# Routing of the second layer with the norm in the row tile, scaling after the ranks and loads one step earlier

## The chip, the cores and the metric

The kernel runs on one core of a Trainium2 chip, as one launch. The metric is the device time of the launch in microseconds (us); the time before is the median of three runs. The engines are TensorE (PE, with its weight loads PEld), VectorE (DVE), ScalarE (ACT), GpSimd (POOL) and SyncE (SP), which issues most of the DMAs.

## What is computed

32 sequences of 256 rows of 128 numbers, 8192 rows in all, pass two layers, all in 32-bit floats. Each layer is `x = x + s * silu(m)`, where `s` is an attention block and `m` a mixture of experts, both of the normed rows.

```
xn = layernorm(x); s = softmax_transformer(xn)          # layer 0, two sublayers
x  = x + s * silu(top8_experts(xn) + shared(xn))        # 64 experts, 64 places each
xn = layernorm(x); s = linear_attention(xn)             # layer 1
topk_ids = argmax(xn @ gate_w); score = sigmoid(max(xn @ gate_w))
g  = silu(shared1(xn) + expert[topk_ids](xn * score))   # 32 experts, one per row
x  = x + s * g
```

The change lies between the two layers and in layer 1: the sum of layer 0, the second layernorm, the choice of the expert (argmax, score), the rank of each row within its expert, and the k and v of the linear attention.

## The kernel before

The rows are worked on in 16 groups (`NG`) of 512 rows, each as four tiles of 128 rows (`GT`). `s_rows` holds for every row 129 numbers: 128 for the row and its own number; `s_all` is the view of the 128.

The kernel has four stages. (1) Layer 0 (L309 to L799) runs in a loop over steps `k` from 0 to 17; in every step several generators are advanced in turn (`run`), so that attention, feed-forward, experts and shared expert are written interleaved. (2) The routing of layer 1 is a generator per group, `begin(g)`: `route(g)` (L178 to L244), followed for groups from 6 (`INL`) by the shared expert `shared1(g)` (L246 to L276). `rolling` runs the groups staggered, a new one after every two steps. Part of it is taken inside steps 15, 16 and 17 of layer 0: 10, 20 and 12 steps (L796 to L798). What is left is drained at L821, after layer 0. (3) Then the place of each row among 96 tiles of experts is computed (`dest`, L824 to L854), and `send` scatters 64 tiles of rows by GpSimd's indirect DMA (L860), while the linear attention (`linear_attention`, L873 to L957) begins. (4) `routed` loads the scattered rows, multiplies them by the experts' weights (L972, L982) and scatters them back (L987), beside the rest of the attention. At the end `finish` adds all up.

`route(g)` has five steps. Step 1 (L182 to L199) loads the two partial sums of the experts and of the shared expert of layer 0 (`c_g`, L185, tag "gate"; `c_m`, L187, tag "chan"), adds them on GpSimd (L188), loads the input rows x (L189), applies silu (by tanh for groups under 8, L192 to L194; as Silu after, L196 and L197) and adds to x (L198). Step 2 norms the rows into a tile `c_xn` of tag "tok": statistics on VectorE (L109, L110), small steps on GpSimd (L111 to L120), the rows on ScalarE (L122). Step 3 transposes them on TensorE (L132) and copies them from PSUM (L204). Step 4 has the logits (L208), the maximum and its index for each row (L216, L217), the mark of the chosen expert `hot` (L221) and the tanh of the score (L223). Step 5 finishes the score (L225), scales the normed rows by it into `s_rows` on GpSimd (L227, four instructions) and computes the ranks (L231 to L243, with the matmuls L235, L236 and L239).

Working tiles come from two pools. `works[0]` has one buffer per tag, `works[1]` two (score and others as noted). Groups 0 to 3 use `works[0]`; later ones use `works[0]` if g is a multiple of 3, and `works[1]` otherwise. Tag "out" is used by `shared1` for its result `f_y`, which ScalarE evicts (L274) and SP stores (L275). The rooms for x of groups 9 to 15 (`room`, L812) are in a pool that takes memory which layer 0 has used, as are the weights of layer 1 (`sw_a`, loaded at L805).

What sets the order: each engine has one queue and takes it in order, and a DMA that must wait on SP holds what stands behind it. The order within a queue is made when the program is built, by a planner that takes the written order as priority but puts ahead what it holds to be ready sooner. So it is near the written order and not the same: six loads of x stand in a row on SP, and the sum of group 15 (L188 at 881.6 us) stands ahead of seven groups' scalings (L227).

In `linear_attention`, k and v of each tile come out of one matmul group of 512 columns (L895) and are evicted with their bias by two VectorE instructions of 256 columns (L896 for `l_k`, L897 for `l_v`). Then follow Silu (L907), the square (L910), its sum per head (L911) and the scaling of k (L917) before the matmuls of L924.

Of the kernel before, what the change touches and what calls it, by code (L numbers as in the profile page):

```python
# [16 lines left out]
F32 = mybir.dt.float32  # L17
I32 = mybir.dt.int32
U32 = mybir.dt.uint32
AF = mybir.ActivationFunctionType  # L20
ALU = mybir.AluOpType
# [4 lines left out]
P = 128  # L26
BATCH, SEQ, D = 32, 256, 128
T = BATCH * SEQ
NT = T // P
GT = 4  # L30
NG = NT // GT
# [4 lines left out]
H1, D1, O1 = 16, 8, 2  # L36
# [24 lines left out]
def recurrent_kernel(ctx: ExitStack, tc: tile.TileContext, x, consts, small0, wsd, wgu, wd, small1, bias1, wr, out):  # L61
    nc = tc.nc
    vec, act, pool, pe, sp = nc.vector, nc.scalar, nc.gpsimd, nc.tensor, nc.sync

    def bcast(ap, axis, n):
        ap = ap.unsqueeze(axis)
        return ap.broadcast_to([n if i == axis else s for i, s in enumerate(ap.shape)])
# [16 lines left out]
    def rows(ap, g):  # L84
        return ap[g * GW : (g + 1) * GW].rearrange("(t p) d -> p t d", p=P)
# [3 lines left out]
    s_all = s_rows[:, :, :D]  # L89
# [8 lines left out]
    half = keep.tile([P, 1], F32, name="half")  # L98
# [29 lines left out]
    def transposed(src):  # L128

        ps = bank("tr", 2)  # L130
        for j in range(GT):
            pe.transpose(ps[:, j * P : (j + 1) * P], src[:, j], ident)  # L132
        return ps
# [11 lines left out]
    at1, x_at, xt_at, hots = {}, {}, {}, {}  # L145
# [6 lines left out]
    def room(pool_, gs):  # L152
        for g in gs:
            x_at[g] = pool_.tile([P, GT, D], F32, name=f"x_{g}")
            xt_at[g] = pool_.tile([P, GW], F32, name=f"xt_{g}")
            if g % 4 == 0:
                hots[g // 4] = pool_.tile([P, NT // 4, E1], F32, name=f"hot_{g // 4}")
# [18 lines left out]
    def work(n):  # L176

        return works[len(works) > 1 and n % 3 > 0]  # L178

    def route(g):  # L180

        wk = works[0] if g < EARLY else work(g)  # L182
        tl = slice(g * GT, (g + 1) * GT)
        gr = wk.tile([P, GT, D], F32, tag="gate", name="c_g")
        sp.dma_start(gr, rows(moe0[0], g))  # L185
        more = wk.tile([P, GT, D], F32, tag="chan", name="c_m")
        sp.dma_start(more, rows(moe0[1], g))  # L187
        pool.tensor_tensor(gr, gr, more, ALU.add)  # L188
        sp.dma_start(x_at[g], rows(x, g))  # L189
        if g < TANH:  # L190

            act.activation(more, gr, AF.Tanh, scale=0.5)  # L192
            vec.scalar_tensor_tensor(gr, more, 1.0, gr, ALU.add, ALU.mult)
            vec.scalar_tensor_tensor(gr, gr, 0.5, s_all[:, tl], ALU.mult, ALU.mult)  # L194
        else:
            act.activation(gr, gr, AF.Silu)  # L196
            vec.tensor_tensor(gr, gr, s_all[:, tl], ALU.mult)  # L197
        vec.tensor_tensor(x_at[g], x_at[g], gr, ALU.add)  # L198
        yield  # L199
        xn = wk.tile([P, GT, D], F32, tag="tok", name="c_xn")  # L200
        normed(wk, x_at[g], xn, act)
        yield
        ps = transposed(xn)
        act.copy(xt_at[g], ps)  # L204
        yield
        lp = bank()
        for j in range(GT):
            pe.matmul(  # L208
                lp[:, j * E1 : (j + 1) * E1], xt_at[g][:, j * P : (j + 1) * P], par1("router"),
                start=True, stop=True,  # L210
            )
        lg = lp[:, : GT * E1].rearrange("p (t e) -> p t e", e=E1)
        m8 = wk.tile([P, GT, 8], F32, name="c_m8")
        i8 = wk.tile([P, GT, 8], U32, name="c_i8")
        for j in range(GT):
            vec.max(m8[:, j], lg[:, j])  # L216
            vec.max_index(i8[:, j], m8[:, j], lg[:, j])  # L217
        fi = wk.tile([P, GT], F32, name="c_fi")
        vec.tensor_copy(fi, i8[:, :, 0])
        hot = hot_of(g)  # L220
        vec.tensor_tensor(hot, bcast(at1["eiota"], 1, GT), bcast(fi, 2, E1), ALU.is_equal)  # L221
        score = wk.tile([P, GT], F32, name="c_sc")
        act.activation(score, m8[:, :, 0], AF.Tanh, scale=0.5)  # L223
        yield
        vec.tensor_scalar(score, score, 0.5, 0.5, ALU.mult, ALU.add)  # L225
        for j in range(GT):
            pool.tensor_scalar(s_all[:, g * GT + j], xn[:, j], score[:, j : j + 1], 0.0, ALU.mult, ALU.add)  # L227


        cum = wk.tile([P, GT, E1], F32, name="c_cum")  # L230
        vec.tensor_copy(cum[:, 0], hot[:, 0])  # L231
        for j in range(1, GT):
            vec.tensor_tensor(cum[:, j], cum[:, j - 1], hot[:, j], ALU.add)
        ps = bank()
        pe.matmul(ps[:, : GT * E1], const("tri"), hot.rearrange("p t e -> p (t e)"), start=True, stop=False)  # L235
        pe.matmul(  # L236
            ps[:, E1 : GT * E1], at1["ones"], cum[:, : GT - 1].rearrange("p t e -> p (t e)"), start=False, stop=True,
        )
        pe.matmul(ps[:, GT * E1 : (GT + 1) * E1], at1["ones"], cum[:, GT - 1], start=True, stop=True)  # L239
        vec.tensor_tensor(at1["before"][:, g + 1], at1["before"][:, g], ps[:, GT * E1 : (GT + 1) * E1], ALU.add)  # L240
        pos = wk.tile([P, GT, E1], F32, name="c_pos")
        vec.tensor_tensor(pos, ps[:, : GT * E1].rearrange("p (t e) -> p t e", e=E1), hot, ALU.mult)
        vec.tensor_reduce(at1["rank"][:, tl], pos, AX.X, ALU.add)  # L243
        yield  # L244

    def shared1(g, home=None):  # L246
# [39 lines left out]
    def drain(i):  # L286
        for _ in i:
            pass
# [20 lines left out]
    with ExitStack() as c0:  # L309
# [3 lines left out]
        wk = c0.enter_context(tc.tile_pool(name="wk0", bufs=2, side="right"))  # L313
# [465 lines left out]
        begun = rolling([begin(g) for g in range(NG)], 2)  # L779
        for k in range(units + 2):  # L780
            if k == 9:
                cf.close()
                works.append(ctx.enter_context(tc.tile_pool(name="first_work", bufs=1)))
                begin1(ctx.enter_context(tc.tile_pool(name="first", bufs=1)))
            if k == 16:
                ca.close()
                works.append(ctx.enter_context(tc.tile_pool(name="mid_work", bufs=2)))
                room(ctx.enter_context(tc.tile_pool(name="mid", bufs=1)), range(EARLY, 9))
            steps = [beside(k), front(k), search(k), share(k)]

            qs = range(sum(working[: max(0, k - FIRST)]), sum(working[: max(0, k - FIRST + 1)]))
            steps += [chain(*(experts(q) for q in qs[i::2])) for i in range(2)]
            if k < units:
                gs, l = unit(k)
                steps = [softmax(gs, l, qkv, k < 9), *steps]
            more = {15: 10, 16: 20, 17: 12}.get(k)  # L796
            if more:
                steps.append(some(begun, more))  # L798
            drain(run(*steps))  # L799


    w1p = ctx.enter_context(tc.tile_pool(name="w1", bufs=1))
    wk = ctx.enter_context(tc.tile_pool(name="wk1", bufs=2))
    t = at1["sw_a"] = w1p.tile([P, cut], F32, name="sw_a")
    sp.dma_start(t, small1[:, :cut])  # L805
    bias = w1p.tile([P, 5 * D], F32, name="bias1")
    sp.dma_start(bias, bias1.broadcast_to([P, 5 * D]))

    vec.tensor_tensor(par1("wq"), par1("wq"), ident, ALU.add)
    wkv4 = par1("wkv").rearrange("p (k d) -> p k d", d=D)  # L810
    vec.tensor_tensor(wkv4, wkv4, bcast(ident, 1, 4), ALU.add)
    room(w1p, range(9, NG))  # L812
    before, rank, ones = at1["before"], at1["rank"], at1["ones"]

    spare = w1p.tile([P, S1], F32, name="spare")
    pool.iota(spare, [[P, S1]], base=T + 1, channel_multiplier=1, allow_small_or_imprecise_dtypes=True)
    siota = w1p.tile([P, 1], F32, name="siota")
    pool.iota(siota, [[0, 1]], base=0, channel_multiplier=P, allow_small_or_imprecise_dtypes=True)

    drain(begun)  # L820


    dest = w1p.tile([P, NT], I32, name="dest")
# [17 lines left out]
    ps = bank()  # L841
# [31 lines left out]
    def linear_attention(g):  # L873

        xt = xt_at[g]
        ps = bank()
# [6 lines left out]
        ps = bank()  # L883
# [3 lines left out]
        qn, kn = norms[:, : GT * H1], norms[:, GT * H1 :]  # L887
        vec.tensor_copy(qn, ps[:, : GT * H1])
        yield

        kf = wk.tile([P, GT, O1 * D], F32, name="l_k")
        vf = wk.tile([P, GT, O1 * D], F32, name="l_v")
        for j in range(GT):
            ps = bank("sc", 4)
            pe.matmul(ps, xt[:, j * P : (j + 1) * P], par1("wkv"), start=True, stop=True)  # L895
            vec.tensor_tensor(kf[:, j], ps[:, : O1 * D], bias[:, : O1 * D], ALU.add)  # L896
            vec.tensor_tensor(vf[:, j], ps[:, O1 * D :], bias[:, O1 * D : 2 * O1 * D], ALU.add)  # L897
            if j % 2:
                yield

# [5 lines left out]
            sp.dma_start(home, rows(moe1, g))  # L906
        act.activation(kf, kf, AF.Silu)  # L907
        k2 = work(g).tile([P, GT * O1 * H1, D1], F32, tag="wide", name="l_k2", bufs=1)
        kflat = kf.rearrange("p t (h d) -> p (t h) d", d=D1)
        act.activation(k2, kflat, AF.Square, bias=half)  # L910
        vec.tensor_reduce(kn, k2, AX.X, ALU.add)  # L911
        next(later, None)
        yield
        act.activation(norms, norms, AF.Sqrt)
        vec.tensor_scalar(norms, norms, 1e-6, None, ALU.add)
        vec.reciprocal(norms, norms)
        vec.scalar_tensor_tensor(kflat, kflat, 0.5, bcast(kn, 2, D1), ALU.add, ALU.mult)  # L917
        next(later, None)
        yield
        ps = bank("tr", 2)  # L920
# [13 lines left out]
        ps = bank()  # L934
# [11 lines left out]
        ps = transposed(o)  # L946
# [3 lines left out]
        ps = bank()  # L950
# [187 lines left out]
```

## Time and profile before

| | before |
|---|---|
| median of 3 runs | 1338.09 us (1333.77 to 1339.4) |
| profiled execution | 1336.66 us, of which the span from first to last instruction is 1334.9 us |
| mean granted TensorE clock | 0.972 |
| PE busy / share of the span | 1222.2 us, 92% |
| DVE, ACT, POOL busy | 943.5 us (71%), 787.6 us (59%), 650.6 us (49%) |
| first and last scatter of the rows (L860) | 942.3 us, 1045.4 us |
| last addition of layer 0 (L688) | 849.3 us |

How to read the profile: it is one execution. The table of stretches gives each engine's busy time in a stretch. A row of waits reads "who, which tile, which line, waited for whom: us in total, how often, the longest". The chain of work that ended last is followed back from the last instruction, at each step to what released it; its rows are start, duration, engine, tile and line. A row of groups gives line, engine and operation, the tiles written and read, their shapes, how often, the busy time in us and the mean of one in ns, and the idle time before it. The granted clock is the share of full speed that TensorE was given.

### The profile page before, as it was taken

How to read it: one execution, taken by the hardware profiler on the slowest of the kernel's cores; microseconds unless marked ns; L12 is line 12 of the kernel's file. 1: busy time of each engine (PE TensorE's matmuls, PEld its weight loads, DVE VectorE, ACT ScalarE, POOL GpSimd, SP SyncE). 2: the span in 40 equal slices, each digit the busy share in tenths (PEclk: the TensorE clock that was granted, in tenths of full speed). 3: DMA queues.
4: the chain of work that ended last, by engine and by line, in shares of the span. 5: the costliest groups of instructions: out<-in, count | busy, mean ns of one | idle time of the engine just before them, and what ended most of it. 6: DMA issues, size and time to landing. Idle time of an engine off the chain costs nothing. (4 is left out here: it accounts for less than half of the span.)

```text
span 1334.9 us, 22827 instructions
## 1 busy us (share of the span) xinstructions
PE 1222.2 (92%) x7425; PEld 863.2 (65%) x7425; DVE 943.5 (71%) x3064; ACT 787.6 (59%) x1858; POOL 650.6 (49%) x1020
## 2 busy tenths in 40 slices
PE   6989999999999899999998877889999899999997
PEld 4546576566566476667666545566566688888873
DVE  4699779879879856656655766776878666676537
ACT  1786666676676567676765766444545465564543
POOL 6362822733722557656644456252477434444540
PEclk9999999999999999999999998989989899999999
DMA  6020301311211332132211133311311366767767
GB/s 183 22 56 25 112 24 48 113 31 41 96 33 40 112 76 59 34 84 56 65 20 34 36 99 94 93 49 40 113 42 45 101 206 199 220 200 220 225 218 207
DMA packets 135078, 125.80 MB, mean 94 GB/s; under 512 B 17104, under 2 KB 110256, under 8 KB 134832
## 3 DMA queue, kind: packets, MB, share of 16 engines
q1 hardware_dynamic: 123696, 108.57, 27.4%
q0 software_dynamic: 11264, 15.78, 4.9%
q8 instruction: 59, 0.97, 0.3%
q14 instruction: 59, 0.48, 0.1%
HBM read 83.63 MB, written 40.68 MB: 93 GB/s over the span
## 5 line engine op out<-in xcount | busy, mean ns | idle before, releaser
L601 ACT ACTIVATE a_pr<-ps_sc,a_nm 128x256 f32<-128x256 f32 x256 | 119.4, 480 | 58.9 <-DVE a_nm L592 58.8
L987 POOL DMA_INDIRECT back<-e_ys,e_toi x96 | 95.1, 991 | 106.3 <-ACT e_ys L986 73.2
L111 POOL TENSOR_SCALAR bn_rs<-bn_mv 128x4 f32<-128x4 f32 x112 | 27.9, 249 | 230.4 <-DVE bn_mv L110 207.0
L663 PE MATMUL ps_mm<-xt,sw 128*128 128x512 f32 x256 | 135.4, 636 | 1.6 <-ACT e_y L523 0.9
L125 POOL TENSOR_SCALAR z<-s_rows,bn_rs 128x128 f32<-128x128 f32 x256 | 129.3, 526 | 6.6
L681 PE MATMUL ps_mm<-sw,m_h 128*128 128x128 f32 x1024 | 128.3, 280 | 2.2 <-ACT e_y L523 1.3
L681 PEld LDWEIGHTS ps_mm<-sw,m_h 128*128 128x128 f32 x1024 | 119.9, 193 | 12.7 <-issue 6.0
L668 DVE SCALAR_TENSOR_TENSOR m_h<-m_h,m_z 128x512 f32<-128x512 f32 x128 | 90.4, 710 | 46.4 <-ACT m_h L667 45.9
L112 POOL TENSOR_TENSOR bn_rs<-bn_rs,power 128x4 f32<-128x4 f32 x112 | 117.4, 1048 | 1.2
L665 ACT ACTIVATE m_z<-ps_mm,fold 128x512 f32<-128x512 f32 x128 | 87.4, 686 | 30.2 <-PE ps_mm L663 29.9
L592 DVE TENSOR_REDUCE a_nm<-ps_sc 128x2 f32<-128x512 f32 x128 | 83.3, 679 | 30.6 <-PE ps_sc L586 30.5
L972 PE MATMUL ps_sc<-e_xt,e_w 128*128 128x128 f32 x768 | 100.8, 278 | 1.0 <-ACT e_xt L1009 0.6
L972 PEld LDWEIGHTS ps_sc<-e_xt,e_w 128*128 128x128 f32 x768 | 94.5, 194 | 9.8 <-issue 7.8
L586 PE MATMUL ps_sc<-a_qk,a_qk 64*128 64x256 f32 x512 | 96.4, 411 | 1.2 <-ACT a_pr L601 1.1
L524 POOL DMA_INDIRECT sums<-e_y,sidx x32 | 51.1, 1598 | 80.4 <-ACT e_y L523 42.7
L618 PE MATMUL ps_tr<-con,a_pr 128*128 128x128 f32 x512 | 76.2, 279 | 9.5 <-ACT a_pt L619 5.6
L618 PEld LDWEIGHTS ps_tr<-con,a_pr 128*128 128x128 f32 x512 | 59.5, 144 | 38.3 <-issue 20.2
L667 ACT ACTIVATE m_h<-m_z 128x512 f32<-128x512 f32 x128 | 80.8, 635 | 1.7
L860 POOL DMA_INDIRECT xslot<-s_rows,dest x64 | 68.4, 1069 | 24.1 <-issue 18.5
L619 ACT COPY a_pt<-ps_tr 128x512 f32<-128x512 f32 x128 | 71.9, 591 | 12.4 <-PE ps_tr L618 11.4
L558 PE MATMUL ps_mm<-xt,sw 128*128 128x512 f32 x128 | 70.3, 657 | 6.4 <-ACT xt L546 3.0
L627 PE MATMUL ps_mm<-a_pt,a_v 128*64 128x256 f32 x512 | 70.9, 396 | 4.2 <-ACT m_z L665 3.6
(236 smaller groups left out, 2950.4 us busy)
## 6 DMA issues: line engine op xcount, KB each, us to landing
e_w<-in_wr_dram SPq DMA_DIRECT2D x96, 384.0 KB, 4.0
xslot<-zero SPq DMA_DIRECT2D x4, 1548.0 KB, 6.7
e_x<-xslot SPq DMA_DIRECT2D x24, 258.0 KB, 3.6
e_wg<-in_wgu_dram SPq DMA_DIRECT2D x16, 384.0 KB, 3.2
x_in<-in_x_dram SPq DMA_DIRECT2D x16, 256.0 KB, 3.2
tab<-s_rows SPq DMA_DIRECT2D x16, 256.0 KB, 2.4
sums<-s_y SPq DMA_DIRECT2D x16, 256.0 KB, 2.3
sums<-zero SPq DMA_DIRECT2D x4, 1024.0 KB, 8.4
```

The costliest lines, as they stand in the source:

```text
L112: pool.tensor_tensor(rs[:, 0], rs[:, 0], power, ALU.pow)
L125: ins = pool.tensor_scalar(dst[:, j], src[:, j], rs[:, 1, j : j + 1], rs[:, 0, j : j + 1], ALU.add, ALU.mult)
L586: pe.matmul(sc[h][:, j * SEQ : (j + 1) * SEQ], qk[0][hd, q0 : q0 + P], qk[1][hd, b * SEQ : (b + 1) * SEQ], start=True, stop=True,)
L592: vec.tensor_reduce(nm[:, 2 * h : 2 * h + 2], sc[h].rearrange("p (j k) -> p j k", k=SEQ), AX.X, ALU.max, negate=True)
L601: act.activation(pr[:, n], sc[h][:, j * SEQ : (j + 1) * SEQ], AF.Exp, bias=nm[:, n : n + 1], accum_out=su[:, n : n + 1],)
L618: pe.transpose(pts[:, n * P : (n + 1) * P], pr[:, n, k * P : (k + 1) * P], ident)
L663: pe.matmul(ps, par("w1", l * FF0 + f * P, P), xt, start=True, stop=True)
L665: act.activation(z, ps, AF.Identity, bias=fold[:, l, 3 + f : 4 + f])
L668: vec.scalar_tensor_tensor(h, h, 1.0, z, ALU.add, ALU.mult)
L681: pe.matmul(ps[:, j * D : (j + 1) * D], hs[f][:, j * P : (j + 1) * P], par("w2", l * FF0 + f * D, D), start=f == 0, stop=f == 3,)
L972: pe.matmul(ps[:, c * P : (c + 1) * P], wt[:, c * P : (c + 1) * P], xt, start=True, stop=True)
L987: ins = pool.indirect_dma_start(out=back, out_offset=bass.IndirectOffsetOnAxis(ap=to, axis=0), in_=ys, in_offset=None,)
```

## The change

Five things are changed.

1. `route(g)`: the two sums are loaded and added one step before they are used (a `yield` moves up), and odd groups use the tags "gate" and "chan", even groups "tok" and "out".
2. The normed rows are written into the row tile `s_rows` itself (no tile `c_xn`), and are scaled there in place by the score, in a step of its own after the ranks. The score gets three buffers.
3. 12, 24 and 16 steps are taken inside layer 0 for 10, 20 and 12; a group has now one step more.
4. The rest is drained before the identity is added to the weights of the attention, and before two small iotas.
5. k and v share one tile `l_kv`, evicted by one instruction of 512 columns; the later instructions read k from it with gaps.

```diff
@@ route
-        gr = wk.tile([P, GT, D], F32, tag="gate", name="c_g")
+        tags = ("gate", "chan") if g % 2 else ("tok", "out")
+        gr = wk.tile([P, GT, D], F32, tag=tags[0], name="c_g")
         sp.dma_start(gr, rows(moe0[0], g))
-        more = wk.tile([P, GT, D], F32, tag="chan", name="c_m")
+        more = wk.tile([P, GT, D], F32, tag=tags[1], name="c_m")
         sp.dma_start(more, rows(moe0[1], g))
         pool.tensor_tensor(gr, gr, more, ALU.add)
         sp.dma_start(x_at[g], rows(x, g))
+        yield
...
         vec.tensor_tensor(x_at[g], x_at[g], gr, ALU.add)
-        yield
-        xn = wk.tile([P, GT, D], F32, tag="tok", name="c_xn")
+        xn = s_all[:, tl]
         normed(wk, x_at[g], xn, act)
...
-        score = wk.tile([P, GT], F32, name="c_sc")
+        score = wk.tile([P, GT], F32, name="c_sc", bufs=3)
...
         vec.tensor_scalar(score, score, 0.5, 0.5, ALU.mult, ALU.add)
-        for j in range(GT):
-            pool.tensor_scalar(s_all[:, g * GT + j], xn[:, j], score[:, j : j + 1], 0.0, ALU.mult, ALU.add)
...
         vec.tensor_reduce(at1["rank"][:, tl], pos, AX.X, ALU.add)
+        yield
+        for j in range(GT):
+            pool.tensor_scalar(xn[:, j], xn[:, j], score[:, j : j + 1], 0.0, ALU.mult, ALU.add)
         yield
@@ layer 0's loop
-            more = {15: 10, 16: 20, 17: 12}.get(k)
+            more = {15: 12, 16: 24, 17: 16}.get(k)
@@ after layer 0
+    room(w1p, range(9, NG))
+    before, rank, ones = at1["before"], at1["rank"], at1["ones"]
+    drain(begun)
     vec.tensor_tensor(par1("wq"), par1("wq"), ident, ALU.add)
     wkv4 = par1("wkv").rearrange("p (k d) -> p k d", d=D)
     vec.tensor_tensor(wkv4, wkv4, bcast(ident, 1, 4), ALU.add)
-    room(w1p, range(9, NG))
-    before, rank, ones = at1["before"], at1["rank"], at1["ones"]
...
-    drain(begun)
@@ linear_attention
-        kf = wk.tile([P, GT, O1 * D], F32, name="l_k")
-        vf = wk.tile([P, GT, O1 * D], F32, name="l_v")
+        kv = wk.tile([P, GT, 2 * O1 * D], F32, name="l_kv")
+        kf, vf = kv[:, :, : O1 * D], kv[:, :, O1 * D :]
...
-            vec.tensor_tensor(kf[:, j], ps[:, : O1 * D], bias[:, : O1 * D], ALU.add)
-            vec.tensor_tensor(vf[:, j], ps[:, O1 * D :], bias[:, O1 * D : 2 * O1 * D], ALU.add)
+            vec.tensor_tensor(kv[:, j], ps, bias[:, : 2 * O1 * D], ALU.add)
...
-        kflat = kf.rearrange("p t (h d) -> p (t h) d", d=D1)
-        act.activation(k2, kflat, AF.Square, bias=half)
+        act.activation(k2.rearrange("p (t n) d -> p t (n d)", t=GT), kf, AF.Square, bias=half)
...
-        vec.scalar_tensor_tensor(kflat, kflat, 0.5, bcast(kn, 2, D1), ALU.add, ALU.mult)
+        k4 = kf.rearrange("p t (h d) -> p t h d", d=D1)
+        vec.scalar_tensor_tensor(k4, k4, 0.5, bcast(kn.rearrange("p (t h) -> p t h", t=GT), 3, D1), ALU.add, ALU.mult)
```

## The prediction, made before the changed kernel ran

> **What bounds the kernel now.** I read first the page's forty slices, for the granted clock, then the busy time by stage, then the waits of TensorE and ScalarE in the stretch the change is about, then the chain through the longest of those waits, and last the groups of the attention's evictions.
>
> From the table of busy time by stretch (start and end in us, then PE, PEld, DVE, ACT, POOL busy, granted clock, DMA share, GB/s):
>
> ```profile
> 700.00:800.00 100.00, 83.05 (x506) 55.99 (x502) 66.33 (x221) 62.80 (x159) 47.72 (x75) 0.93 0.21 54
> 800.00:850.00 50.00, 40.15 (x230) 30.75 (x231) 33.27 (x143) 27.57 (x56) 24.69 (x42) 0.87 0.23 68
> 850.00:900.00 50.00, 41.63 (x181) 27.27 (x181) 36.41 (x205) 20.61 (x47) 26.19 (x48) 0.86 0.34 94
> 900.00:950.00 50.00, 46.96 (x266) 33.21 (x265) 37.09 (x177) 20.39 (x42) 16.94 (x35) 1.00 0.24 72
> 1100.00:1150.00 50.00, 47.34 (x354) 41.03 (x353) 34.99 (x105) 29.34 (x62) 23.04 (x28) 1.00 0.70 209
> ```
>
> TensorE carries the kernel: 47 of 50 us in the last stage. Only from 720 to 890 us is it clearly idle (16.95 us in 700 to 800, 9.85 in 800 to 850, 8.37 in 850 to 900), and there its clock is low too. In this stretch layer 0 ends and the routing of layer 1 (L178 to L244) runs in its shadow until 849.3 us, then alone with the shared expert until 942.3 us, when the first scatter of L860 starts. So the change can win at most what TensorE loses in this stretch, and a little later.
>
> The waits there, who for whom, us in total, times, longest; first for 700 to 850 us, then for 840 to 945 us:
>
> ```profile
> PE ps_tr L132 <- ACT c_xn L122: 9.5, 4, 6.8
> ACT c_xn L122 <- POOL s_rows L227: 11.1, 5, 3.5
> ```
>
> ```profile
> PE ps_tr L132 <- ACT c_xn L122: 2.0, 3, 1.1
> ACT c_xn L122 <- POOL s_rows L227: 14.5, 7, 3.3
> POOL s_rows L227 <- DVE c_sc L225: 17.5, 4, 7.0
> ```
>
> ScalarE cannot write the next group's normed rows `c_xn` before GpSimd has scaled the last ones out of the same buffer (L227), and GpSimd cannot scale before the score is there. TensorE, whose queue is in order, stands at the transpose behind them. The longest case in the chain that ended last:
>
> ```profile
> 799.63 2.49 POOL s_rows L227 x3
> 802.14 0.50 ACT c_xn L122
> 802.69 0.86 PE ps_tr L132 x2
> ```
>
> The statistics of that group were ready long before: its last small GpSimd step (L120) started at 780.75 and took 0.20 us, yet the row was written at 802.14.
>
> **The change, part by part.** The sum is made against the profiled execution: span 1334.9 us, 1336.66 us with what lies around it, 1.43 us below the median of 1338.09.
>
> *The norm goes into the row tile, scaled later in place.* Removed: the buffer `c_xn`, so the wait of ScalarE for L227 (11.1 + 14.5 = 25.6 us by the two views, some counted twice where they overlap). Nothing is added: 64 normalisations of 479 ns and 64 scalings of 382 ns stay what they are. Of the 25.6 us, TensorE shows 9.5 + 2.0 = 11.5 us as its own. In the 6.8 us case not all comes back: the next layer-0 norm's `z` (L125) ended only at 795.5, and after it stand a transpose (0.6 us), a copy (0.59) and the next matmul, so about 2.3 us of latency stay. I take two thirds of 9.5, that is 6 us, and 1 us of the 2.0.
>
> *The clock.* The granted clock was 0.63 in 795 to 800, 0.50 in 800 to 805, 0.85 in 805 to 810: 1.85 + 2.5 + 0.75 = 5.1 us lost around that one stall. In 862 to 890 it was 0.82, 0.50, 0.83, 1.00, 0.57, 0.88 and 0.70 in steps of 4 us: 6.8 us lost. Here the Trainium skill ("TensorE: Matmul & The Clock Gate", Part 1 and its table of goals) speaks against counting the second: the clock falls to half after an idle window of about 3.4 us, and gaps below about 3 us should not cost it. The longest listed stall in 840 to 945 is 2.0 us, and the clock was still 0.50 in 866 to 870. By the rule the clock saving there is 0; by the row it is up to 6.8 us. The measurement decides, but the short stalls that remain (VectorE's chain of maxima before L235) will still pull it down. I take 2 us of the 5.1, and 1 us of the 6.8.
>
> *The scaling a step behind the ranks.* The four L227 of a group no longer stand in GpSimd's queue before the score is there. Behind them stood the next norm's L111 to L120 (0.2 + 1.02 + 0.2 + 0.2 us). GpSimd is busy 26 of 50 us, so the 17.5 us of waiting is mostly idle time that cost nothing; what it cost is the `c_xn` wait already counted: 0 more. Its cover is the scatter stage: if scalings slid past 942 us they would stand ahead of scatters, 1.5 us a group. The last one ended at 936.6, so I take 0, at worst 1.5.
>
> *The sums a step ahead, in two pairs of tags.* The same 48 loads, now one step earlier. GpSimd's add (L188, 1.27 us) waited for the two loads 5.6 + 1.7 = 7.3 us in all, in stretches in which TensorE had layer-0 work: 0 to 2 us, I take 0. Each load is issued past what stands on SP; the block at the weight load L805 (14.9 + 5.4 us of waiting, until 849.3) stays where it is, and so do the x loads of groups 9 to 15, whose room only opens there (850.2 to 857.9). So the seven last groups cannot start earlier.
>
> *More steps taken within layer 0 (12, 24, 16 for 10, 20, 12).* 52 steps of seven per group against 42 of six: 7.4 against 7.0 groups. Group 6's rank, group 7's transpose and group 8's load come inside. Their TensorE work (1.2 + 0.6 us) falls into idle time: a gain of 0 to 2. Against it, one GpSimd add (1.27 us) and one norm (about 1.9 us) may come ahead of layer 0's `z` on the chain: a loss of 0 to 3. I take 0.
>
> *The drain put before the additions of the identity.* L809 and L811 (0.29 + 0.67 us on VectorE) waited only 0.2 us for data. They come after the drain now; VectorE is busy 10.0 of 10 us in 940 to 950, ahead of the first scatter. Gain 0.2, loss at most 0.97: I take 0. The two iotas that go with them (0.35 us) waited 8.2 us for released memory, with only L227 behind: 0.
>
> *One eviction for k and v.* Groups, with count, busy us and mean ns:
>
> ```profile
> L896 DVE TENSOR_TENSOR l_k<-ps_sc,bias x64: 355/418/426, 947.0 to 1296.6; 128x256 f32<-128x256 f32 x64
> L897 DVE TENSOR_TENSOR l_v<-ps_sc,bias x64: 402/414/418, 947.4 to 1297.0; 128x256 f32<-128x256 f32 x64
> L954 DVE TENSOR_TENSOR s_rows<-ps_mm,bias 128x512 f32<-128x512 f32 x16 | 11.0, 689 | 2.9 <-PE ps_mm L952 2.6
> ```
>
> (The first two show least, median and greatest ns.) The nearest row for 512 columns out of PSUM is L954 at 689 ns: 418 + 414 - 689 = 143 ns saved, times 64 = 9.2 us of VectorE. VectorE is busy about 35 of 50 us there, TensorE 47, so most is beside the path. TensorE's waits for VectorE in 1050 to 1300 are 6.9 us (`e_hs`) and 2.5 us (`l_o`). VectorE's load falls by 9.2 of the 227 us of 950 to 1300, 4%; I take a quarter of those waits, 2 us. Against it, k is ready 0.27 us later after the last matmul of a group (0.689 for 0.418), at the Silu of L907; on the path only for the last group: 0.3 us. k is read with gaps by ScalarE and VectorE afterwards (L907, L910, L917); no row shows a cost of that. Bounds: 0 (the s_rows reads, also with gaps, are no slower than others: L197 689 ns, L954's kind) and 5% of the three (1.06 + 1.15 + 1.22 us, 16 times) = 2.7 us, mostly beside the path. I take 0.
>
> Sum: -6 - 1 - 2 - 1 - 2 + 0.3 = about -11.5 us. Span 1334.9 - 11.5 = 1323.4, its execution 1325.2, the median of runs **1327** (rounded from 1326.6).
>
> **The rivals.** *A, the stalls are refilled (no change).* Between 890 and 940 us TensorE is already 97% busy at full clock (48.4 of 50), and the seven last groups start only when the memory of layer 0 comes free at 849. If the time won before that goes into waits for layer 0's own chain (norm, widen, tanh, narrow), and the drain keeps VectorE's chains, only the 2 us of k and v are left: 1336. For it: TensorE's waits for the next activations in the same stretch (a_pt 5.6 us, z 2.4). Against: the 6.8 us stall is ahead of layer-0 work in one queue.
>
> *B, slower: a load behind a store.* Today tag "out" serves only the shared expert's result `f_y`; now the second sum of even groups uses it too. For group 14 it is the pool of two buffers, shared with the `f_y` of groups 7, 8, 10 and 11. SP waited 61.6 us for `f_y` (L275) between 884 and 941, and behind it stood no load, since the last was issued at 875.6. In the new kernel group 14's load can stand there. From its issue to its rank I add the rows: 2.9 landing, 1.27 add, 0.63 silu, 1.4 product and sum, 1.5 statistics, 1.9 small steps, 1.65 rows, 0.6 transpose, 0.59 copy, 1.0 logits, 2.5 maxima, 2.2 to the rank: 18 us; then group 14's and 15's shared part, 6 us each, partly open. Issued behind the `f_y` of 909.0 it would have its rank by 928, before today's last one (937.5): no loss. Behind the one of 916.8 it is at 936, and about 8 us of TensorE work comes after it that today is done beside: from about 912 us on it decides. Price +8 to +14, nothing else gained: 1346 to 1352.
>
> *C, more is won.* If TensorE's idle time in 795 to 890 halves, with its clock: 10 us of idle and 6 of clock on top of 2, about -20 with the rest: 1317, down to 1308.
>
> **How the numbers follow.** Main case 0.48, A 0.20, B 0.22, C 0.10. About 0.5% (6.7 us) is what a measurement of this kernel can tell from no change: under 1331.4 is faster, over 1344.8 slower. Faster: nearly all of the main case (0.44) and C: 0.54. Same: 0.04, A's 0.18 and a little of B: 0.23. Slower: 0.23. The main case alone spans 1319 to 1333. The range 1308 to 1349 reaches to C's end and into B.
>
> **What would show it.** Right: no wait of ScalarE's L122 for the scaling; TensorE's stall at 795 to 802 gone with the clock near 1 there; 64 evictions near 690 ns for 128; the first scatter 8 to 10 us earlier than 942.3. A: the same waits gone, the first scatter at 940 or later. B: a load of `c_m` issued after 912 us behind an `f_y` store, TensorE idle before the last ranks. Wrong altogether would be a later end of layer 0 (today's last L688 at 849.3), for which I have only the 0 to 3 us above.

## The result and the profile after

| | before | after |
|---|---|---|
| median of 5 runs each, side by side | 1336.29 us (1333.77 to 1339.4) | 1330.73 us (1325.38 to 1332.34) |
| ratio, 95% interval | | 0.9945 [0.9927, 0.9964] |
| span of the profiled execution, mean clock | 1334.9 us, 0.972 | 1323.6 us, 0.978 |
| last addition of layer 0 | 849.3 us | 845.4 us |
| first and last scatter of the rows | 942.3, 1045.4 us | 932.4, 1034.6 us |
| logits of the sixth group begin | 849.1 us | 843.4 us |

The kernel is 0.55% faster. The profiled execution of after is the fastest of its five (1325.38 us), so the two spans differ by 11.3 us and the medians by 5.6 us. The 11.3 us are 3.9 at the end of layer 0, another 6.0 by the first scatter, 0.9 by the last scatter and 0.5 after it. The kernel after has other line numbers: scaling L245, rank matmul L234, widening and narrowing matmuls of layer 0 L665 and L683, last addition L690, scatter L863, matmul and eviction of k and v L898 and L899.

The table of stretches of the kernel after (columns as before):

```profile
700.00:800.00 100.00, 86.39 (x531) 60.20 (x528) 67.89 (x226) 66.30 (x168) 50.15 (x78) 0.91 0.21 56
800.00:850.00 50.00, 41.38 (x228) 29.77 (x228) 38.65 (x161) 26.10 (x55) 27.67 (x44) 0.86 0.33 91
850.00:900.00 50.00, 42.51 (x210) 29.28 (x210) 35.66 (x208) 19.75 (x46) 22.92 (x50) 0.90 0.26 73
1100.00:1150.00 50.00, 47.72 (x359) 41.77 (x359) 31.32 (x83) 28.40 (x60) 23.61 (x27) 1.00 0.74 222
```

TensorE's idle time in 700 to 900 is 13.61 + 8.62 + 7.49 = 29.7 us, where it was 35.2. Its clock did not rise: length times (1 - granted clock), over the three rows, is 9 + 7 + 5 = 21.0 us, where it was 7 + 6.5 + 7 = 20.5. In this stretch the gain is idle time filled, not a higher clock. Over the whole span TensorE's idle time fell from 112.7 us (1334.9 - 1222.2 busy) to 104.3 us (1323.6 - 1219.3).

The waits, first of the kernel after for 700 to 850 us, then of the same for 840 to 945 us, then one row of the kernel before for 700 to 850 us:

```profile
ACT s_rows L122 <- POOL bn_rs L120: 19.3, 7, 4.2
POOL c_g L189 <- DMA c_g<-sums: 17.6, 3, 9.1
...
PE ps_mm L665 <- ACT m_z L667: 5.2, 3, 4.0
...
PE ps_tr L132 <- ACT s_rows L122: 4.0, 2, 2.3
```

```profile
ACT s_rows L122 <- POOL bn_rs L120: 10.3, 6, 2.5
...
PE ps_tr L132 <- ACT s_rows L122: 5.5, 4, 3.1
```

```profile
PE ps_mm L663 <- ACT m_z L665: 0.4, 1, 0.4
```

The wait of ScalarE for the scaling, 11.1 and 14.5 us, has no row any more. In its place ScalarE waits for GpSimd's last norm step (L120), 19.3 and 10.3 us. TensorE's own waits for the normed rows went from 9.5 + 2.0 to 4.0 + 5.5 us: 2.0 us less, not the 7 that I had taken. And a wait came in that the kernel before hardly has: in layer 0's widening TensorE waits 5.2 us for ScalarE (`m_z`), for 0.4 before. The longest case, 4.0 us, ends at 746.75. There ScalarE stood 4.22 us at a row of the route's norm, waiting for L120, with layer 0's activation behind it in its queue; and GpSimd had run an addition of the sums (L189, 1.26 us at 741.62) just ahead of that norm's small steps. So whatever made the kernel faster, it is not simply that wait. The stall itself did leave the place where it stood. TensorE's instructions in the timeline, first before, then after (start, duration, then idle time before and its releaser):

```profile
802.69 0.86 PE L132 MATMUL ps_tr<-con,c_xn 128*128 128x128 f32 x2 [6.76 <-ACT c_xn L122]
...
804.20 1.06 PE L681 MATMUL ps_mm<-sw,m_h 128*128 128x128 f32 x4
...
819.47 1.11 PE L663 MATMUL ps_mm<-xt,sw 128*128 128x512 f32 x2
```

```profile
797.46 0.33 PE L132 MATMUL ps_tr<-con,z 128*128 128x128 f32 x1 [2.02 <-POOL z L125]
...
800.21 7.14 PE L683 MATMUL ps_mm<-sw,m_h 128*128 128x128 f32 x60
807.33 0.49 PE L234 MATMUL ps_mm<-hot,con 128*128 128x128 f32 x2
...
812.09 2.05 PE L665 MATMUL ps_mm<-xt,sw 128*128 128x512 f32 x2
```

Where it stood still from 795.9 to 802.7 before, it now transposes and computes logits, and from 800.2 it runs 60 narrowing matmuls of layer 0 in a row, with the group's rank matmul only behind them. The next widening of layer 0 (L665) starts at 812.1, where it was 819.5. Stretches of 5 us, first of before, then of after:

```profile
795.00:800.00 5.00, 0.72 (x3) 0.28 (x2) 2.54 (x7) 1.95 (x4) 4.10 (x6) 0.63 0.49 117
800.00:805.00 5.00, 2.31 (x10) 2.06 (x11) 3.72 (x16) 2.21 (x5) 2.43 (x4) 0.50 0.72 211
```

```profile
795.00:800.00 5.00, 2.88 (x23) 2.25 (x22) 2.09 (x5) 2.97 (x6) 4.81 (x9) 1.00 1.01 281
800.00:805.00 5.00, 4.99 (x45) 4.80 (x45) 4.89 (x20) 2.20 (x5) 3.00 (x3) 1.00 1.18 290
810.00:815.00 5.00, 4.10 (x14) 2.36 (x12) 3.82 (x25) 0.63 (x1) 2.72 (x4) 0.53 0.04 10
815.00:820.00 5.00, 4.00 (x9) 2.16 (x10) 3.29 (x18) 4.09 (x10) 3.15 (x7) 0.50 0.23 69
```

From 795 to 805 us the clock is 1.00 where it was 0.63 and 0.50; from 810 to 820 us it is 0.53 and 0.50 where it was 1.00. The dip has moved.

### The profile page after: what moved, and what is told of

Read it like the earlier page. It is cut to its first block, busy times and chain, and to the rows that moved or that the text cites. A ratio compares the mean times of both kernels' runs of the same rounds, so it can differ in the third digit from the quotient of the medians.

```text
span 1323.6 us, 22753 instructions
## 1 busy us (share of the span) xinstructions
PE 1219.3 (92%) x7425; PEld 859.7 (65%) x7425; DVE 941.1 (71%) x3000; ACT 785.8 (59%) x1858; POOL 649.2 (49%) x1020
## 5 line engine op out<-in xcount | busy, mean ns | idle before, releaser
L665 PE MATMUL ps_mm<-xt,sw 128*128 128x512 f32 x256 | 136.9, 640 | 6.5 <-ACT m_z L667 5.2
L683 PE MATMUL ps_mm<-sw,m_h 128*128 128x128 f32 x1024 | 126.0, 278 | 1.4 <-ACT e_y L525 1.3
L683 PEld LDWEIGHTS ps_mm<-sw,m_h 128*128 128x128 f32 x1024 | 118.3, 192 | 11.0 <-issue 5.5
L620 PEld LDWEIGHTS ps_tr<-con,a_pr 128*128 128x128 f32 x512 | 60.3, 145 | 38.4 <-issue 20.5
L621 ACT COPY a_pt<-ps_tr 128x512 f32<-128x512 f32 x128 | 71.8, 591 | 12.7 <-PE ps_tr L620 11.7
L863 POOL DMA_INDIRECT xslot<-s_rows,dest x64 | 66.0, 1031 | 24.7 <-issue 18.5
L560 PE MATMUL ps_mm<-xt,sw 128*128 128x512 f32 x128 | 72.3, 673 | 6.2 <-ACT xt L548 3.0
```

Of the source, the lines that this page charges most:

```text
L620: pe.transpose(pts[:, n * P : (n + 1) * P], pr[:, n, k * P : (k + 1) * P], ident)
L665: pe.matmul(ps, par("w1", l * FF0 + f * P, P), xt, start=True, stop=True)
L683: pe.matmul(ps[:, j * D : (j + 1) * D], hs[f][:, j * P : (j + 1) * P], par("w2", l * FF0 + f * D, D), start=f == 0, stop=f == 3,)
L863: ins = pool.indirect_dma_start(out=xslot, out_offset=bass.IndirectOffsetOnAxis(ap=dest[:, t : t + 1], axis=0), in_=s_rows[:, t], in_offse ...
```

## The experiments

Each ratio is to the kernel before, measured beside it on the same chip; the kernel before itself took 1350.57, 1353.91 and 1335.58 us in the three groups, so only ratios are compared between groups. Timelines come from one profiled execution of each kernel.

### First group: what is each part worth?

**One eviction for k and v, alone**, in the kernel before:

```diff
...
-            vec.tensor_tensor(kf[:, j], ps[:, : O1 * D], bias[:, : O1 * D], ALU.add)
-            vec.tensor_tensor(vf[:, j], ps[:, O1 * D :], bias[:, O1 * D : 2 * O1 * D], ALU.add)
+            vec.tensor_tensor(kv[:, j], ps, bias[:, : 2 * O1 * D], ALU.add)
...
```

> The kernel before with one eviction for k and v as its only edit. My theory (the gain comes from the routing; k and v are worth 2 us): ratio to before 0.998 to 1.000, the first scatter where it was (942 us, within 1), VectorE busy about 9 us less. Rival (the gain comes from the attention's evictions, the stage in which TensorE is fullest): ratio 0.994 to 0.996, and the stretch from the first scatter to the end is shorter by 5 us or more.

Ratio 1.0002 [0.9984, 1.002]. It is worth nothing.

**The change without it**: the kernel after with the two evictions back (the diff above, reversed).

> The changed kernel with the two evictions of 256 columns put back. My theory: ratio to before 0.995 to 0.997 (most of the 0.9945 stays), the first scatter near 932 as in the changed kernel. Rival (the evictions carry it): ratio 0.999 to 1.001.

Ratio 0.9944 [0.9921, 0.9967]: the whole gain, without this part.

**In place, alone**: in the kernel before, the normed rows go into the row tile and are scaled there, at the old place in the order.

```diff
-        xn = wk.tile([P, GT, D], F32, tag="tok", name="c_xn")
+        xn = s_all[:, tl]
...
-            pool.tensor_scalar(s_all[:, g * GT + j], xn[:, j], score[:, j : j + 1], 0.0, ALU.mult, ALU.add)
+            pool.tensor_scalar(xn[:, j], xn[:, j], score[:, j : j + 1], 0.0, ALU.mult, ALU.add)
```

> The kernel before with one edit: the normed rows go into the row tile and are scaled there, at the old place right after the score. My theory (the wait of ScalarE for the scaling is what cost): no wait of ScalarE's L122 for the scaling, TensorE's 6.8 us stall gone, ratio to before 0.994 to 0.997. Rival (the stalls are refilled, or the gain needs the scaling a step later and the earlier loads): ratio 0.999 to 1.002, with the first scatter at 940 us or later.

Ratio 1.0091 [1.006, 1.0121]: slower. The part on which most of my sum stood costs 0.9% by itself. TensorE's timeline in that kernel shows how (its lines here: rank matmul L235, narrowing L681, widening L663):

```profile
801.72 1.95 PE L132 MATMUL ps_tr<-con,s_rows 128*128 128x128 f32 x8
808.39 0.80 PE L235 MATMUL ps_mm<-hot,con 128*128 128x128 f32 x2 [4.72 <-DVE hot L221]
808.97 1.92 PE L681 MATMUL ps_mm<-sw,m_h 128*128 128x128 f32 x8
...
829.15 1.02 PE L663 MATMUL ps_mm<-xt,sw 128*128 128x512 f32 x2
```

The stall for the normed rows is gone. But route steps still stand ahead of layer 0's narrowing matmuls in TensorE's queue, and now the next of them, the rank matmul, waits 4.72 us for `hot` from VectorE, until 808.4 where the stall of before ended at 802.7. This wait follows an earlier one:

```profile
788.49 0.49 ACT L122 ACTIVATE s_rows<-x,bn_rs 128x128 f32<-128x128 f32 x1 [4.86 <-POOL bn_rs L120]
```

```profile
790.12 1.84 PE L663 MATMUL ps_mm<-xt,sw 128*128 128x512 f32 x2 [3.82 <-ACT m_z L665]
```

With no buffer to wait for, a row of the route's norm stands in ScalarE's queue ahead of layer 0's activation, waits there 4.86 us for GpSimd, and holds TensorE 3.82 us. The last transposes of layer 0's `z` begin at 798.9 for 793.8 before, and the logits behind them, from which `hot` is made, at 800.4 for 791.2. Layer 0's widening starts at 829.2 (before 819.5), layer 0 ends at 857.6 (849.3), and the memory for the last groups comes free then. After it TensorE has little to do. Stretches of 20 us in that kernel:

```profile
860.00:880.00 20.00, 11.74 (x55) 10.02 (x54) 13.51 (x85) 3.83 (x11) 11.10 (x22) 0.66 0.60 164
880.00:900.00 20.00, 14.28 (x54) 10.34 (x55) 10.38 (x45) 9.77 (x22) 9.31 (x14) 0.66 0.14 40
```

26.0 of 40 us busy at a clock of 0.66; the kernels before and after have 31.7 and 32.9 us busy in the 40 us that follow their layer 0. From 700 us to the first scatter, first before, then in place alone:

```profile
700.00:942.30 242.30, 205.63 (x1154) 143.88 (x1151) 165.41 (x716) 127.99 (x299) 109.37 (x193) 0.92 0.23 63
```

```profile
700.00:955.10 255.10, 214.55 (x1166) 151.62 (x1165) 170.98 (x715) 126.74 (x300) 108.53 (x192) 0.89 0.22 59
```

The first scatter comes 12.8 us later. TensorE is idle 40.6 us for 36.7, and loses about 28 us for 19 to the clock by the measure used above. So the larger part of the delay is busy time, 8.9 us more of it, which fits the lower clock; idle time is the smaller part.

**Tags back**: the kernel after with the tags "gate" and "chan" for every group; the loads stay a step ahead.

```diff
-        tags = ("gate", "chan") if g % 2 else ("tok", "out")
+        tags = ("gate", "chan")
```

> The changed kernel with both sums in the tags gate and chan for every group again (loads still a step ahead), so that no load shares a buffer with the store of the shared expert. Rival B of the prediction (a load behind a store costs): faster than the changed kernel, ratio to before 0.991 to 0.993. My theory: the tags are worth 0 to 2 us, so 0.994 to 0.997, with GpSimd waiting longer for the sums.

Ratio 0.9972 [0.9958, 0.9986], against 0.9944 [0.9921, 0.9967] of the change without the eviction in the same group. The second pair of tags brings about 0.3% at most: the intervals overlap.

### Second group: does the later scaling repair it, or the step counts?

**The scaling a step later, alone**, in the kernel before (out of `c_xn`):

```diff
-        for j in range(GT):
-            pool.tensor_scalar(s_all[:, g * GT + j], xn[:, j], score[:, j : j + 1], 0.0, ALU.mult, ALU.add)
...
         vec.tensor_reduce(at1["rank"][:, tl], pos, AX.X, ALU.add)
+        yield
+        for j in range(GT):
+            pool.tensor_scalar(s_all[:, g * GT + j], xn[:, j], score[:, j : j + 1], 0.0, ALU.mult, ALU.add)
```

> The kernel before with one edit: the scaling in a step of its own after the ranks, still from the separate buffer c_xn (held longer). My theory: the wait of ScalarE for the buffer grows, ratio 1.000 to 1.006. Rival (the block in GpSimd's queue was the whole cost, and the buffer's wait was beside it): ratio 0.994 to 0.998.

Ratio 1.0004 [0.9984, 1.0025]: nothing.

**In place and later together**, both edits above in the kernel before:

> The kernel before with two edits: the norm in the row tile, and its scaling in a step of its own after the ranks. In place alone had the ratio 1.0091, with GpSimd waiting at the scaling for the score ahead of the next norm. My theory now (the scaling a step later takes that block out of GpSimd's queue, so both edits are needed together): ratio 0.994 to 0.998, the waits of the scaling L227's kind for the score's makers below 40 us. Rival (in place costs by itself, since routing work gets ahead of layer 0's end; what repairs it in the changed kernel is the loads or the step counts): ratio 1.003 to 1.010, and layer 0's last addition at 855 us or later.

Ratio 1.0092 [1.0057, 1.0126], no better than in place alone. My theory after the first group, that GpSimd's scalings ahead of the norms cost the 0.9% and that scaling later takes them away, falls. The stall is again the rank matmul's:

```profile
811.00 0.80 PE L233 MATMUL ps_mm<-hot,con 128*128 128x128 f32 x2 [6.20 <-DVE hot L221]
...
833.44 1.02 PE L664 MATMUL ps_mm<-xt,sw 128*128 128x512 f32 x2
```

**Step counts back**: the kernel after with the old counts of route steps inside layer 0.

```diff
-            more = {15: 12, 16: 24, 17: 16}.get(k)
+            more = {15: 10, 16: 20, 17: 12}.get(k)
```

> The changed kernel with 10, 20 and 12 steps inside layer 0 again. My theory (the counts are worth nothing by themselves): within 0.2% of the changed kernel. Rival (what is taken inside layer 0 sets when its memory comes free and what is left to cover the start of the last groups): off by 0.3% or more from the changed kernel, with layer 0's last addition moved by 3 us or more.

Ratio 1.0078 [1.0053, 1.0103], while **the kernel after again** in the same group gave 0.9966 [0.9944, 0.9988]. Inside the new kernel the three numbers are worth about 1.1%, twice the whole gain. With the old counts, the kernel with all other parts of the change is slower than before.

The old numbers do not bring back the old share of routing, though, because a group has now one step more. Counted in the program, 42 steps of the kernel before write groups 0 to 5, group 6 to its logits and group 7 to its norm inside layer 0. In the new kernel 42 steps end at the norm of group 6, and 52 finish group 6, transpose group 7 and load group 8. The amount alone is not what costs: the later scaling alone has 42 of these longer steps too, and its ratio is 1.0004.

> The changed kernel as it is, beside the others on one chip: ratio 0.993 to 0.997. Rival for the single evictions (they help once the routing is shorter, though alone they measured 1.0002): clearly below the 0.9944 of the changed kernel without them, 0.991 to 0.993.

TensorE's timeline with the old counts (widening L665):

```profile
820.15 1.91 PE L665 MATMUL ps_mm<-xt,sw 128*128 128x512 f32 x2
825.11 0.86 PE L132 MATMUL ps_tr<-con,s_rows 128*128 128x128 f32 x2 [3.04 <-ACT s_rows L122]
...
829.68 2.05 PE L665 MATMUL ps_mm<-xt,sw 128*128 128x512 f32 x2 [0.47 <-DVE c_pos L241]
```

Transposes of a route group, waiting 3.04 us for their rows, its logits and its rank matmuls stand between layer 0's first and second pair of widening matmuls, which start 9.5 us apart. In the kernel after of this group they start 4.8 us apart:

```profile
816.14 2.05 PE L665 MATMUL ps_mm<-xt,sw 128*128 128x512 f32 x2
...
820.97 1.92 PE L665 MATMUL ps_mm<-xt,sw 128*128 128x512 f32 x2
```

Layer 0 then ends at 854.4 (849.8 in the kernel after of this group), and in the next 40 us TensorE is busy 25.9 us, where it is 33.0 in the kernel after. First the old counts, then the kernel after:

```profile
854.40:894.40 40.00, 25.89 (x114) 19.65 (x112) 24.24 (x151) 11.44 (x28) 18.37 (x39) 0.70 0.29 78
```

```profile
849.80:889.80 40.00, 32.95 (x155) 21.81 (x154) 28.95 (x159) 16.26 (x38) 18.29 (x40) 0.91 0.35 91
```

### Third group: is it the shared expert's matmuls?

In two kernels that lose, the new one with the old counts and the one in place and later, TensorE ran 10 and 15 matmul instructions of layer 1's shared expert (gate and up) before the end of layer 0; in the kernel after none. (The profile shows two instructions for one matmul of the program. The kernel before has 8 there, in place alone 20.) They might delay layer 0's end, and then be missing as work after it. Three kernels hold these matmuls behind layer 0's last narrowing matmul, by an order on TensorE's queue alone:

```diff
-                    pe.matmul(
+                    narrowed[:] = [pe.matmul(
...
+                if home is None and g < 9:
+                    tc.add_manual_dep(ins.ins, narrowed[-1].ins.name, order, reason="after layer 0's last")
```

**Held, with the old counts:**

> The changed kernel with 10, 20 and 12 steps (ratio 1.0078, 10 such matmuls ahead, last addition at 854.4), with the same order added. My theory: what the counts do is done through the planner's order at this place, so the ratio comes back to 0.994 to 0.999. Rival (the counts matter by the routing steps themselves, which would stand outside layer 0): ratio 1.004 or more.

Ratio 1.0028 [1.0008, 1.0048]: about half of the loss is back (1.0078 without the order). TensorE has more work after layer 0:

```profile
854.90:894.90 40.00, 30.91 (x142) 22.34 (x141) 28.66 (x169) 13.58 (x34) 17.34 (x40) 0.83 0.32 85
```

but layer 0 still ends at 854.9.

**Held, in place and later:**

> The kernel with the norm in the row tile and the scaling a step later (ratio 1.0092, 15 matmuls of the shared expert ahead of layer 0's last addition, which came at 859.0 us), with one added edit: the gate and up matmuls of the shared expert of groups 6 to 8 are ordered behind layer 0's last matmul on TensorE. My theory (they delay the release of layer 0's memory, on which the last seven groups wait, and are missing afterwards as cover): layer 0's last addition back at 846 to 851, TensorE over 31 of the 40 us after it busy, ratio 0.995 to 1.000. Rival (in place or the later scaling slow the routing by themselves): ratio stays at 1.006 or more.

Ratio 1.0139 [1.0098, 1.0179], no better than 1.0092 without the order (the intervals overlap). Layer 0 ends at 856.6 (859.0 without holding); the rank matmul's wait of 6.2 us is there as before:

```profile
PE ps_mm L233 <- DVE hot L221: 7.0, 2, 6.2
```

**Held, in the kernel before:**

> The kernel before (8 such matmuls ahead, last addition at 849.3) with the same order added and nothing else. My theory: a part of the change's gain without the change: ratio 0.995 to 0.999, last addition 2 to 4 us earlier. Rival (the gain is that of the buffer's wait taken away): 0.999 to 1.002.

Ratio 1.0024 [1.0003, 1.0045]: no gain from holding alone, with 0 of these matmuls ahead of layer 0's end, which stays at 848.4.

So the shared expert's matmuls do not make layer 0 end late: in the two losing kernels it still ends 5.6 and 7.3 us later than in the kernel before, without them. As work that is missing afterwards they are a part of the loss with the old counts, and no measured part of the loss in place.

**More steps still**, the kernel after with 18 steps in the last place for 16:

```diff
-            more = {15: 12, 16: 24, 17: 16}.get(k)
+            more = {15: 12, 16: 24, 17: 18}.get(k)
```

> The changed kernel with 18 steps in the last round for 16, so that group 7's logits and group 8's norm are written inside layer 0 as well. If more steps inside are better as such: ratio 0.991 to 0.994. My theory (16 already has no shared matmul ahead, so there is nothing more to win): within 0.3% of the changed kernel's 0.9966 to 0.9945.

Ratio 0.9953 [0.9927, 0.9979], as the change itself. The counts have no further gain in this direction.

## Why the prediction was right, and where its steps were wrong

The predicted 1327 us lies 3.7 us below the measured 1330.7, the side is right, and the signs that I had named came: no wait of L122 for the scaling, the stall at 795 to 802 gone with the clock at 1.00 there, the first scatter 9.9 us earlier (rival A wanted it at 940 or later). But the gain is about half of what I forecast, 5.6 us side by side for 11.5, and that it is there at all is partly luck: two large terms were wrong, in opposite directions. (The terms as listed add to 11.7, not 11.5.)

*The norm into the row tile, -6 and -1.* This step failed as a term of its own. I argued that an instruction of TensorE that no longer waits gives its time to what stands behind it. The run with this part alone is 0.9% slower, some 12 us. The time went to two other waits: 3.82 us for `m_z`, since the freed norm stands in ScalarE's queue ahead of layer 0's activation, and 4.72 us at the rank matmul, the next instruction of the routing, which waits for its own input. What stood behind, the narrowing matmuls of layer 0, began at 809.0 and not at 804.2. These waits and the lower clock after them are in the trace; that they are the reason for the whole 0.9% was argued from the order of events, not isolated. "Nothing is added" was true of the work and not of the queues.

*The step counts, 0.* This failed most. Between 52 and 42 of the longer steps lie about 1.1%, some 15 us, where I had a "gain of 0 to 2" and a "loss of 0 to 3". My term compared 7.4 groups with the 7.0 of the kernel before, the run with 42 longer steps takes in 6.0, so the two are not the same question; but I counted only the work that the steps bring along (a rank, a transpose, a load). What the traces show to change is the order around layer 0's last chain, that is, which route matmuls stand ahead of the widening and narrowing ones. That this order is the cause is argued. The rest of the change without the counts is 0.8% slower than before; with them the change is 0.3 to 0.6% faster. The counts alone in the kernel before were not run, so their worth outside this change is open.

*The clock, -2 and -1.* Wrong: 20.5 us lost before and 21.0 after. The dip of 795 to 805 went, but came at 810 to 820. The rule of the Trainium skill that I had weighed ("TensorE: Matmul & The Clock Gate", Part 1 and its table of goals: no idle gaps over about 3 us between bursts of matmuls, else half clock) fits one dip and not two others. Stretches of 4 us in the kernel after:

```profile
858.00:862.00 4.00, 1.04 (x2) 0.21 (x2) 1.76 (x9) 1.01 (x2) 2.84 (x5) 0.94 0.01 2
862.00:866.00 4.00, 3.84 (x8) 1.78 (x9) 2.61 (x12) 1.95 (x6) 2.26 (x4) 0.50 0.00 0
```

The longest wait of TensorE listed in 840 to 945 is 3.1 us, about the rule's limit of 3 us, and the clock is halved in the 4 us that follow. There it agrees. The dip at 866 to 870 before, with no listed wait above 2.0 us, it doesn't explain, nor the one that came at 810 after, ahead of which TensorE's longest idle time since 800 us was 0.77 us:

```profile
808.00:809.00 1.00, 0.46 (x2) 0.30 (x2) 1.00 (x3) 0.63 (x1) 1.00 (x2) 1.00 1.06 316
809.00:810.00 1.00, 0.60 (x5) 0.60 (x6) 0.96 (x6) 0.63 (x1) 0.56 (x2) 1.00 0.66 185
810.00:811.00 1.00, 0.96 (x7) 0.79 (x6) 0.95 (x5) 0.00 (x0) 1.00 (x1) 0.66 0.03 8
```

TensorE is only half busy there, for 2 us, before the clock falls. Where rule and row differ the row decides; no run settles what sets it.

*The scaling behind the ranks, 0.* Right: 1.0004 alone.

*The sums a step ahead and the tags, 0.* Nearly right for the tags: about 0.3% at most, at the edge of what is measured. The earlier sums were not run alone. GpSimd's addition waits longer for its loads, 17.6 + 3.5 us (first load and second) in 700 to 850 for 5.6 + 1.7; what that costs was not isolated. A load behind a store, as in rival B, is there: the last such load was issued at 897.1 behind a store of `f_y`, for which it waited 3.5 us. It came before the 912 us from which B decides, and taking away the sharing gave no gain.

*One eviction, -2 + 0.3.* The duration was right, the worth wrong. The group row of after:

```profile
L899 DVE TENSOR_TENSOR l_kv<-ps_sc,bias x64: 671/687/693, 937.2 to 1285.3; 128x512 f32<-128x512 f32 x64
```

687 ns (689 taken) for 418 + 414, so VectorE has 64 x 145 ns = 9.3 us less to do, and the kernel gains nothing by it (ratio 1.0002). TensorE is busy 47 of 50 us in that stage in both kernels: a quarter of its small waits was too much. Reading k with gaps is free, as taken: the Silu, the square, the sum and the scaling take 1057, 1150, 1220 and 1214 ns (1057, 1152, 1219 and 1216 before).

*The end of layer 0, unmoved.* It came 3.9 us earlier. I had named a later end as what would make the prediction wrong altogether, and the kernels that lose by being in place do end it late. But it is not what makes the gain. All profiles, TensorE's idle time counted from 700 us to the first scatter:

| kernels | ratio | end of layer 0 | first scatter | TensorE idle |
|---|---|---|---|---|
| after, after again, without the eviction, tags back, more steps | 0.9944 to 0.9972 | 844.7 to 849.8 us | 929.8 to 935.6 us | 31.0 to 33.9 us |
| before, and those that keep `c_xn` (eviction alone, later alone, held) | 1 to 1.0024 | 848.4 to 850.3 us | 940.4 to 944.6 us | 36.7 to 37.8 us |
| in place alone; in place and later, also held; old counts, also held | 1.0028 to 1.0139 | 854.4 to 859.0 us | 946.8 to 955.1 us | 38.6 to 43.7 us |

The first two rows overlap in the end of layer 0 and not in the first scatter: the gaining kernels need 85.1 to 87.0 us from the one to the other, all others 90.1 to 97.5. By these profiles, one of each kernel, the gain is made mostly in the routing that runs after layer 0.

*The drain put before the identity, 0,* was not run alone and stays untested.

What stays open is why the order comes out well with 12, 24 and 16 and badly with 10, 20 and 12. An order of TensorE's queue fixed by hand between 795 and 835 us, in the old kernel and in the new, would tell whether it is the order alone; it was not tried, and neither were 48 steps, which with the longer groups give the old share. No kernel tried was faster than the one after beyond what is measured: 0.9944 without the eviction and 0.9953 with more steps are equal to its 0.9945.

## What to carry to other kernels

In an in-order queue a removed wait pays only as far as the next instruction of the same chain is ready: look there before the time is booked, and ask whether other work stands between. Look too at what the freed instruction now stands ahead of in its own engine's queue: here a norm that no longer waited for a buffer waited for GpSimd instead, in front of layer 0's activation. Where a planner makes the order, a small change of how much is written into a stage is an edit in its own right, to be costed from both sides by the stall that it can put ahead of the chain that frees the next stage's memory; and when a step is split, count again what the same number of steps takes in. Time saved on an engine that isn't the limit of its stage, as the 9.3 us of VectorE here, is worth nothing until a wait on the limiting engine is shown to end with it.

## What was not expected of the hardware

The time from the first to the last scatter was 103.1 and 102.2 us in the profiles of before and after, and 115.0 us in that of the one eviction alone, which differs from before by it alone. There GpSimd waited longer for VectorE's statistics (first before, 942 to 1046 us, then the one eviction alone, 941 to 1060 us):

```profile
POOL bn_rs L111 <- DVE bn_mv L110: 9.0, 2, 7.2
```

```profile
POOL bn_rs L111 <- DVE bn_mv L110: 22.0, 4, 8.3
```

The kernel after, profiled a second time in the second group, also took 119.8 us for it (935.6 to 1055.4). All profiles of the first two groups took 109.5 to 122.3 us, and there the kernel before ran 1.1 to 1.3% longer; the four of the third group, where it ran 1335.58 us, took 102.3 to 105.5 us. So the difference comes with the group rather than with the code. The first and the third group carry the same chip number (10, the second 9), which speaks for the moment and against the chip; the cause isn't settled.
